# A convolution and a whitening pass: y written over x in four tiles, and pieces of one image in the last pass

## The chip, the cores and the metric

The kernel runs on one core of one Trainium2 chip. The metric is the device time of one execution in microseconds. Five engines work side by side: TensorE (PE in the profile), VectorE (DVE), ScalarE (ACT), GpSimd (POOL) and SyncE (SP). SP only issues DMAs here; 16 DMA engines move the bytes.

## The reference, cut to what matters

```python
# x: (4 images, 64 channels, 256, 256) float32
# layer 0: a separable filter from two small sine networks, hx and hy
k   = einsum('ijk,imk->ijmk', hx, hy)           # 256 x 256 taps per channel
y   = irfft2(rfft2(x, 512) * rfft2(k, 512) / 512)[..., :256, :256]   # causal 2-D convolution
y   = y + x * bias
# layer 1: whitening over channels
x1  = transpose(y, (1, 0, 2, 3)).reshape(64, -1)
s   = x1[:, ::9]                                # every ninth pixel
cov = s @ s.T / s.shape[1] + 0.01 * eye(64)
W   = five Newton-Schulz steps towards cov ** -0.5
out = W @ (x1 - mean(s))                        # for all pixels
```

Since the filter is an outer product, the convolution is done as two products with Toeplitz matrices, one along each image axis. The second layer needs W before the first output can be written, and W needs samples of all four images. So y goes to device memory and comes back in a last pass.

## The kernel before, in words

**Steps and groups.** The channels are cut into 8 blocks g of 8, and a step is one block of one image, (g, n): 32 steps, numbered i. The first 24 steps walk over g = 0 to 5 with all four images in each; the last eight are ordered by image, so steps 24 and 25 finish image 0, 26 and 27 image 1, 28 and 29 image 2, 30 and 31 image 3. A step has four items, one for each pair of channels c = 0, 2, 4, 6. An item needs two products; `group(first, second)` runs the first product of one item beside the second product of the item two before it. I write (i, c) for the group that starts with item (i, c). After the products, ScalarE copies the half results (line 396), and VectorE forms y = x * bias + product (`scalar_tensor_tensor`, line 399). `store` then sends the pair of channels to `y_d` in device memory (line 411).

**The order** of the engines' work is written out by hand (`manual_schedule`). All loads and the stores of y stand on SP's queue, which is worked off in order: a DMA whose wait is not over holds back all that is queued behind it. After each group come, in this order: the store of the item just finished, one load of x, perhaps a block of a Toeplitz matrix (`blocks`), and perhaps a piece of the last pass (`early`).

**Tiles.** The pool `big` holds three x tiles (tag `in`) and three y tiles (tag `out`) of 16 KB per partition each; every step takes the next of each. Three Toeplitz tiles and four sample tiles have the same size, so there are 13 slots of 16 KB. At (i, c) the x of step i + 2 is loaded, its last pair at (i + 1, 0).

**Samples and covariance.** When a step's last pair is stored, nine masked copies (`pack_ops`, line 313) are queued; VectorE takes about three of them after each group. They read the y tile, so it comes free only after them. `covariance(n)` runs on TensorE one image later, ahead of group (27, 4), (29, 4) and (31, 4), and at the end.

**The last pass.** After the chain that computes W, 32 pieces of 128 rows by 4096 pixels (2 MB) are read from `y_d`, multiplied by W on TensorE, shifted on ScalarE and VectorE in place, and stored from GpSimd's queue (line 598). A piece holds 4096 pixels of two images: its rows are the 64 channels of image 2v and the 64 of image 2v + 1. `homes` names the slot of each piece in turn; piece i + 13 is loaded (line 351) when piece i has been stored. Eight pieces are loaded in the loop at the places of `early`, which are (28, 4), (28, 6), (29, 6), (30, 4), (31, 2), (31, 4) and twice (31, 6), the other five of the first 13 right after it.

Of the kernel before, what the change touches and what calls it, by code (L numbers as in the profile page):

```python
# [37 lines left out]
F32 = mybir.dt.float32  # L38
# [6 lines left out]
NB, C, L = 4, 64, 256  # L45
P, H2 = 128, 2
EMB, ORDER = 33, 64
PIX = L * L
CG = 8
# [7 lines left out]
FP = 4096  # L57
# [8 lines left out]
def conv_whiten_kernel(ctx: ExitStack, tc: tile.TileContext, a: dict, out: bass.AP):  # L66
    nc = tc.nc
    x = a["x"]

    const = ctx.enter_context(tc.tile_pool(name="const", bufs=1))  # L70
    big = ctx.enter_context(tc.tile_pool(name="big", bufs=3))
    spool = ctx.enter_context(tc.tile_pool(name="spool", bufs=NB))
    tpool = ctx.enter_context(tc.tile_pool(name="tpool", bufs=3))
    o1pool = ctx.enter_context(tc.tile_pool(name="o1pool", bufs=4))
    dram = ctx.enter_context(tc.tile_pool(name="dram", bufs=1, space=bass.MemoryType.DRAM))
    psA = ctx.enter_context(tc.tile_pool(name="psA", bufs=8, space=bass.MemoryType.PSUM))

    y_d = [dram.tile([2 * C, PIX], F32, tag=f"y{v}", name=f"y_d{v}") for v in range(NB // 2)]
    g_d = dram.tile([P, GW], F32, tag="g", name="g_d")
    g0_d = dram.tile([2, GW], F32, tag="g0", name="g0_d")  # L80

    scratch = big.tile([P, 16, L], F32, tag="out", name="scratch")

    zw = scratch[0:EMB, 13:15, :].rearrange("p a w -> p (a w)")[:, 0 : L + P]
    nc.sync.dma_start(out=zw, in_=a["zw"])
# [8 lines left out]
    bias = const.tile([P, C], F32, tag="bias", name="bias")  # L96
    nc.scalar.dma_start(out=bias, in_=a["bias"].partition_broadcast(P))

    def new_x(g, n):
        return big.tile([P, CG, H2, L], F32, tag="in", name=f"x_{g}_{n}")  # L100

    def load_x(t, g, n, c):
        nc.sync.dma_start(
            out=t[:, c : c + 2],
            in_=x[n, g][:, c : c + 2],
        )
# [1 line left out]

    steps = [(g, n) for g in range(C // CG - 2) for n in range(NB)]
    steps += [(g, n) for n in range(NB) for g in range(C // CG - 2, C // CG)]  # L110
    loaded = {s: new_x(*s) for s in steps[:2]}
    for c in range(0, CG, 2):
        load_x(loaded[steps[0]], *steps[0], c)

    ident = const.tile([P, P], F32, tag="ident", name="ident")
    make_identity(nc, ident)
# [143 lines left out]

    def half_group(item, which):

        g, n, c, xt, yt, o1s = item
        jobs = []
        for u in range(2):
            banks = [
                psA.tile([P, L], F32, tag="psA", name=f"ph{which}_{g}_{n}_{c + u}_{m}")
                for m in range(H2)
            ]
            jobs.append((banks, (o1s[u] if which else xt[:, c + u]), toep[g][:, which, c + u, :]))  # L270
        toeplitz_alone(jobs, which)
        if which == 0:
            for u in range(2):
                o1s.append(o1pool.tile([P, H2, L], F32, tag="o1", name=f"o1_{g}_{n}_{c + u}"))
        for m in range(H2):
            for u in range(2):
                ps = jobs[u][0][m]
                if which == 0:
                    copy = nc.vector.tensor_copy if u else nc.scalar.copy
                    for to, fr in ((slice(0, HP), slice(HP, P)), (slice(HP, P), slice(0, HP))):  # L280
                        copy(o1s[u][to, m], ps[fr])  # L281
                else:
                    ch = g * CG + c + u
                    nc.vector.scalar_tensor_tensor(  # L284
                        yt[:, c + u, m], xt[:, c + u, m], bias[:, ch : ch + 1], ps,
                        ALU.mult, ALU.add,
                    )

# [32 lines left out]
    def covariance(n):  # L321
# [13 lines left out]
        nc.vector.scalar_tensor_tensor(cov, pc, 1.0 / NSAMP, cov, ALU.mult, ALU.add)  # L335


    pieces = [(v, q) for v in range(NB // 2) for q in range(PIX // FP)]


    homes = [
        {"t": (tpool, "toep"), "s": (spool, "samp"), "i": (big, "in"), "o": (big, "out")}[k]
        for k in "tssioitsoitos"
    ]

    def load_y(i):

        v, q = pieces[i]
        pool, tag = homes[i % len(homes)]
        t = pool.tile([P, FP], F32, tag=tag, name=f"yi_{v}_{q}")  # L350
        nc.sync.dma_start(out=t, in_=y_d[v][:, q * FP : (q + 1) * FP])
        return t

    def load_next():
        loaded[len(loaded)] = load_y(len(loaded))

    loaded_x, loaded = loaded, {}
    todo = []
    pending = []

# [8 lines left out]
            k = first + (part * 12 // 8 if g < C // CG - 2 else part)  # L369
            blocks[k // 4, k % 4 * 2] = (g, part)  # L370

    early = {(28, 4): 1, (28, 6): 1, (29, 6): 1, (30, 4): 1, (31, 2): 1, (31, 4): 1, (31, 6): 2}
    orders = [list(range(L // HP)), list(reversed(range(L // HP)))]

    def pack(time=math.inf):
# [5 lines left out]
    def group(first, second):  # L381

        units = []
        g1, n1, c1, x1, _, o1s1 = first
        g2, n2, c2, x2, y2, o1s2 = second
        for u in range(2):
            job2 = (bank(f"p2_{g2}_{n2}_{c2 + u}"), o1s2[u], toep[g2][:, 1, c2 + u, :])
            job1 = (bank(f"p1_{g1}_{n1}_{c1 + u}"), x1[:, c1 + u], toep[g1][:, 0, c1 + u, :])
            units.append((job1, job2))

        toeplitz_products(units, orders[0])
        orders.reverse()
        for u in range(2):
            o1 = o1pool.tile([P, H2, L], F32, tag="o1", name=f"o1_{g1}_{n1}_{c1 + u}")
            for to, fr in ((slice(0, HP), slice(HP, P)), (slice(HP, P), slice(0, HP))):
                nc.scalar.copy(o1[to], units[u][0][0][fr])  # L396
            o1s1.append(o1)
            ch = g2 * CG + c2 + u
            nc.vector.scalar_tensor_tensor(  # L399
                y2[:, c2 + u], x2[:, c2 + u], bias[:, ch : ch + 1], units[u][1][0],  # L400
                ALU.mult, ALU.add,
            )

        pack(2.5)
        store(second)

    def store(second):
        g, n, c, _, yt, _ = second
        last = (g, n) == steps[-1]
        row = n % 2 * C + g * CG + c  # L410
        nc.sync.dma_start(
            out=y_d[n // 2][row : row + 2, :].rearrange(
                "c (b p w) -> p (c b) w", p=P, w=L
            ),
            in_=yt[:, c : c + 2].rearrange("p c b w -> p (c b) w"),
        )
        if last and c == CG // 2 - 2 or not last and c == CG - 2:
            todo.extend(pack_ops(g, n, yt, slice(0, c + 2)))

    engines = mybir.EngineType  # L420
    with tc.manual_schedule(
        engines={engines.PE, engines.SP, engines.DVE, engines.Activation, engines.Pool}
    ):
        toep = {0: new_toeplitz(0)}

        for f, lo, hi in ((0, 0, 2), (0, 2, 4), (0, 4, 6), (1, 0, 2), (0, 6, 8), (1, 2, 4), (1, 4, 8)):
            for half in range(2):
                load_toeplitz(toep[0], 0, f, half, lo, hi)
        for c in range(0, CG, 2):
            load_x(loaded_x[steps[1]], *steps[1], c)  # L430
        for i, (g, n) in enumerate(steps):
            xt = loaded_x.pop((g, n))
            yt = big.tile([P, CG, H2, L], F32, tag="out", name=f"y_{g}_{n}")
            for c in range(0, CG, 2):
                item = (g, n, c, xt, yt, [])
                if g == C // CG - 1 and n > 0 and c == 4:
                    covariance(n - 1)
                if len(pending) == 2:
                    group(item, pending.pop(0))
                else:  # L440
                    half_group(item, 0)
                pending.append(item)
                if i == 0 and c == 6:

                    fold = const.tile([P, C], F32, tag="fold", name="fold")
                    nc.vector.tensor_tensor(fold, ident[:, 0:C], ident[:, C:P], ALU.add)
                    twice = const.tile([C, 2, C], F32, tag="twice", name="twice")
                    for u in range(2):
                        nc.vector.tensor_copy(twice[:, u], ident[0:C, 0:C])

                part = (c - 2) // 2 % 4
                to = i + 2 if c else i + 1
                if to < len(steps) and to > 1:
                    if part == 0:
                        loaded_x[steps[to]] = new_x(*steps[to])
                    load_x(loaded_x[steps[to]], *steps[to], 2 * part)
                if (i, c) in blocks:
                    tg, part = blocks[i, c]
                    if part == 0:
                        toep[tg] = new_toeplitz(tg)  # L460
                    lo = part % 2 * CG // 2
                    load_toeplitz(toep[tg], tg, part // 4, part // 2 % 2, lo, lo + CG // 2)
                for _ in range(early.get((i, c), 0)):
                    load_next()
        g, n, c, xt, yt, _ = pending[0]
        for item in pending:
            half_group(item, 1)
            pack(1.0)
            store(item)

        pack()
        pack_by_pe(g, n, yt, slice(CG // 2, CG))
        covariance(NB - 1)
        while len(loaded) < len(homes):
            load_next()
# [92 lines left out]


    halves = [slice(u * C, (u + 1) * C) for u in range(2)]  # L570
    for i, (v, q) in enumerate(pieces):
        yt = loaded.pop(i)
        o = out[2 * v : 2 * v + 2].rearrange("u c h w -> (u c) (h w)")[:, q * FP : (q + 1) * FP]

        part = FP if 1 < i < len(pieces) - 2 else FP // 4
        for w in range(FP // 1024):


            po = [
                psA.tile([P, 512], F32, tag="psA", name=f"po_{v}_{q}_{w}_{u}") for u in range(2)  # L580
            ]
            cols = [slice((2 * w + k) * 512, (2 * w + k + 1) * 512) for k in range(2)]
            for k in range(2):
# [73 lines left out]
```

## Time and profile before

| what | value |
|---|---|
| median of 3 runs | 918.35 us (917.23 to 919.46) |
| profiled execution, its own time | 917.19 us |
| its span | 915.2 us |
| mean granted TensorE clock | 0.946 |
| busy: TensorE, VectorE, ScalarE | 789.1, 658.2, 479.2 us |
| moved by DMA | 285.57 MB, mean 312 GB/s |
| loads of x: number, size, issue to landing | 128, 512 KB, 5.5 us |
| stores of y | 128, 512 KB, 4.2 us |
| pieces read, pieces written whole | 32 and 28, 2048 KB, 16.4 and 44.3 us |

The span runs from the first to the last instruction; the profiled execution's own time has about 2 us around it. A busy share is a mean over stages with different limits, so the stages are looked at one by one: a row of slices gives the busy tenths in 40 equal parts of the span, and a table by stage gives busy time, clock and DMA rate for chosen stretches. Idle time of an engine that does not set the end costs nothing.

### The profile page before, as it was taken

The numbers are of one execution on the slowest core, as the hardware profiler recorded it, in microseconds if no ns is written. First come the engines' busy times: TensorE is split into PE (matmuls) and PEld (weight loads), VectorE is DVE, ScalarE is ACT, GpSimd is POOL, SyncE is SP. The second block draws the span as 40 slices with busy tenths as digits, with TensorE's granted clock in tenths as the row PEclk, the third lists the DMA queues.
The fourth block names the chain that finished last, engine by engine and source line by source line (L and its number), as shares of the span: only waits on it lengthen the run. The fifth ranks groups of instructions, "written<-read, shape, count | busy, mean of one in ns | idle before, by whom it ended". The sixth has DMA issues, their size and how long they took to land.

```text
span 915.2 us, 27979 instructions
## 1 busy us (share of the span) xinstructions
PE 789.1 (86%) x11876; PEld 633.3 (69%) x11876; DVE 658.2 (72%) x882; ACT 479.2 (52%) x791; POOL 31.7 (3%) x71
## 2 busy tenths in 40 slices
PE   8999999999999999999999999997877777765500
PEld 7999999999999999999999999996311111111100
DVE  3468776877687768786878666867599999986500
ACT  2545454545454545454545444540498888866400
POOL 3000000000000000000000000000110000000010
PEclk9999999999999999999999999998699999987655
DMA  4988888798888888889997769989999999999998
GB/s 152 304 282 260 248 259 271 229 273 261 246 263 261 246 260 260 257 249 279 278 274 232 236 192 364 326 276 406 416 404 431 428 430 430 430 430 430 429 433 347
DMA packets 115499, 285.57 MB, mean 312 GB/s; under 512 B 6925, under 2 KB 89264, under 8 KB 107696
## 3 DMA queue, kind: packets, MB, share of 16 engines
q1 hardware_dynamic: 108176, 216.08, 71.0%
q0 software_dynamic: 6336, 67.11, 17.3%
q8 instruction: 94, 1.54, 0.7%
q10 hardware_dynamic: 864, 0.60, 0.2%
q14 instruction: 29, 0.24, 0.1%
HBM read 149.35 MB, written 134.42 MB: 310 GB/s over the span
## 4 chain that ended last, share of the span: by engine, by line
PE 68%; issue 15%; DVE 13%; DMA 1%; POOL 1%; ACT 0%; ACTq 0%; POOLq 0%; DVEq 0%
PE p L215 63%; DVE yi L593 12%; PE pc L327 2%; PE ph L247 1%; PE pk L295 1%; DMA mask<-in_mask_dram 1%; POOL pick L131 1%; PE po L585 1%; POOL out_dram L598 0%; DMA toep<-g_d 0%; DVE y L284 0%; PE ZY L500 0%; PE YT L500 0%; ACT L518 0%; DMA g_d<-scratch 0%
## 5 line engine op out<-in xcount | busy, mean ns | idle before, releaser
L215 PE MATMUL p<-toep,o 64*64 64x64 f32 (+3 forms) x5040 | 578.5, 284 | 0.2 <-issue 0.2
L215 PE MATMUL p<-toep,x 64*64 64x64 f32 (+3 forms) x5040 | 578.5, 284 | 0.1
L215 PEld LDWEIGHTS p<-toep,x 64*128 64x128 f32 (+1 forms) x5040 | 533.9, 166 | 23.4 <-issue 0.3
L215 PEld LDWEIGHTS p<-toep,o 64*128 64x128 f32 (+1 forms) x5040 | 535.2, 166 | 10.7 <-issue 0.4
L396 ACT COPY o<-p 64x512 f32<-64x512 f32 x504 | 292.4, 580 | 297.7 <-PE p L215 289.9
L313 DVE COPY_PREDICATED samp<-mask,y 128x448 f32<-128x448 int32 (+3 forms) x288 | 281.2, 976 | 6.6
L399 DVE SCALAR_TENSOR_TENSOR y<-x,bias,p 128x512 f32<-128x512 f32 x252 | 177.4, 743 | 138.7 <-PE p L215 138.1
L593 DVE TENSOR_SCALAR yi<-po,shift 64x512 f32<-64x512 f32 x256 | 192.0, 750 | 24.8 <-PE po L585 18.5
L585 PE MATMUL po<-yi,W 64*64 64x512 f32 x1024 | 152.4, 668 | 62.4 <-DVE yi L593 39.4
L590 ACT ACTIVATE yi<-po,shift 64x512 f32<-64x512 f32 x256 | 174.9, 683 | 43.9 <-PE po L585 36.8
L585 PEld LDWEIGHTS po<-yi,W 64*64 64x64 f32 x1024 | 36.8, 145 | 177.2 <-DVE yi L593 123.3
L598 POOL DMA_DIRECT2D out_dram<-yi x44 | 23.6, 537 | 263.2 <-DMA out_dram<-yi 115.4
L484 POOL MEMSET chain<- 64x64 f32 x1 | 0.1, 144 | 603.2 <-PE ph L247 603.2
L327 PEld LDWEIGHTS pc<-samp 128*64 128x64 f32 x464 | 14.3, 137 | 1.8 <-issue 1.0
L327 PE MATMUL pc<-samp 128*64 128x65 f32 x464 | 14.9, 223 | 0.4 <-ACT samp L304 0.4
L150 PE MATMUL busy<-idle 128*128 128x128 f32 x94 | 13.0, 301 | 0.0
L150 PEld LDWEIGHTS busy<-idle 128*128 128x128 f32 x94 | 12.4, 216 | 0.2 <-issue 0.2
L281 DVE COPY o<-ph 64x256 f32<-64x256 f32 x8 | 3.4, 421 | 9.1 <-PE ph L247 8.9
L295 PE MATMUL pk<-y,pick 128*128 128x112 f32 (+1 forms) x36 | 7.7, 388 | 2.6 <-DVE y L284 2.6
L335 DVE SCALAR_TENSOR_TENSOR cov<-pc,cov 128x65 f32<-128x65 f32 x4 | 0.9, 227 | 12.1 <-PE pc L327 12.1
L295 PEld LDWEIGHTS pk<-y,pick 128*128 128x128 f32 x36 | 7.2, 258 | 2.8 <-issue 2.7
L281 ACT COPY o<-ph 64x256 f32<-64x256 f32 x8 | 2.9, 367 | 10.0 <-PE ph L247 9.9
(81 smaller groups left out, 80.3 us busy)
## 6 DMA issues: line engine op xcount, KB each, us to landing
x<-in_x_dram SPq DMA_DIRECT2D x128, 512.0 KB, 5.5
y_d<-y SPq DMA_DIRECT2D x128, 512.0 KB, 4.2
yi<-y_d SPq DMA_DIRECT2D x32, 2048.0 KB, 16.4
out_dram<-yi POOLq DMA_DIRECT2D x28, 2048.0 KB, 44.3
out_dram<-yi POOLq DMA_DIRECT2D x16, 512.0 KB, 9.8
toep<-g_d SPq DMA_DIRECT2D x29, 256.0 KB, 6.6
toep<-g_d SPq DMA_DIRECT2D x29, 192.0 KB, 5.8
toep<-g_d SPq DMA_DIRECT2D x6, 128.0 KB, 3.2
```

Of the source, the lines that this page charges most:

```text
L131: nc.gpsimd.tensor_scalar(pick[:, s, :], ident, rows[:, s : s + 1], None, ALU.mult)
L150: nc.tensor.matmul(p, lhsT=idle[:, 0:P], rhs=idle[:, P : 2 * P], start=True, stop=True)
L215: mm = nc.tensor.matmul(ps[q : q + w, m, HP * k : L], lhsT=src[parts, k // 2, m * P + q : m * P + q + w], rhs=t[parts, : stop : -1] if k e ...
L295: nc.tensor.matmul(pk[:, b, :, 0:nj], lhsT=pick[:, (s - b) % STEP, :], rhs=yt[:, cs, b, s : s + STEP * (nj - 1) + 1 : STEP], start=(s == 0 ...
L313: nc.vector.copy_predicated(dst, m, src)
L327: nc.tensor.matmul(pc[half], lhsT=samp[n][:, b, j, 0:C], rhs=samp[n][:, b, j, :], start=(b == 0 and j < 2), stop=(b == H2 - 1 and j >= NJ ...
L396: nc.scalar.copy(o1[to], units[u][0][0][fr])
L399: nc.vector.scalar_tensor_tensor(y2[:, c2 + u], x2[:, c2 + u], bias[:, ch : ch + 1], units[u][1][0], ALU.mult, ALU.add,)
L585: nc.tensor.matmul(po[u][halves[k]], lhsT=W[halves[u]], rhs=yt[halves[u], cols[k]], start=True, stop=True,)
L590: nc.scalar.activation(yt[halves[0], cols[k]], po[0][halves[k]], AF.Identity, bias=shift[halves[k]])
L593: nc.vector.tensor_scalar(yt[halves[1], cols[k]], po[1][halves[k]], shift[halves[k]], None, ALU.add)
L598: nc.gpsimd.dma_start(out=o[:, end - part : end], in_=yt[:, end - part : end])
```

## The change

The pool `big` becomes `xpool` with four tiles and `epool` with two. The multiply-add of VectorE writes y over x in the same tile (the argument `yt` goes). Step i works in place i % 4 up to step 26, and in place i % 3 from step 27 on, so that the fourth tile is free for a piece. At (i, c) the pair c of step i + 2 is loaded up to step 24; step 25 loads none; from step 26 on pair c of step i + 1 is loaded. `y_d` becomes one tensor for each image, with 64 channels of the upper and 64 of the lower half as its 128 rows, so a store of two channels becomes two DMAs, one for each half, and a piece holds one image. `homes` gets the two `extra` slots first. Nine pieces are loaded in the loop, the first two at (26, 4) and (26, 6), and four right after it. The output tensor has the same order of rows, and the host puts the halves back in place after the device has finished.

```diff
-    big = ctx.enter_context(tc.tile_pool(name="big", bufs=3))
+    xpool = ctx.enter_context(tc.tile_pool(name="xpool", bufs=4))
+    epool = ctx.enter_context(tc.tile_pool(name="epool", bufs=2))
...
-    y_d = [dram.tile([2 * C, PIX], F32, tag=f"y{v}", name=f"y_d{v}") for v in range(NB // 2)]
+    y_d = [dram.tile([H2 * C, PIX // H2], F32, tag=f"y{n}", name=f"y_d{n}") for n in range(NB)]
...
+    x_tiles = {
+        u: xpool.tile([P, CG, H2, L], F32, tag="in", name=f"x{u}") for u in (3, 2, 0, 1)
+    }
+
+    def place_of(i):
+        return i % 4 if i < 27 else i % 3
...
-    pieces = [(v, q) for v in range(NB // 2) for q in range(PIX // FP)]
+    pieces = [(n, q) for n in range(NB) for q in range(PIX // H2 // FP)]
...
-        for k in "tssioitsoitos"
+        for k in "eeitssistiits"
...
-    early = {(28, 4): 1, (28, 6): 1, (29, 6): 1, (30, 4): 1, (31, 2): 1, (31, 4): 1, (31, 6): 2}
+    early = {
+        (26, 4): 1, (26, 6): 1, (27, 0): 1, (27, 2): 1, (27, 6): 1, (29, 6): 1, (31, 0): 1, (31, 4): 2
+    }
...
             nc.vector.scalar_tensor_tensor(
-                y2[:, c2 + u], x2[:, c2 + u], bias[:, ch : ch + 1], units[u][1][0],
+                x2[:, c2 + u], x2[:, c2 + u], bias[:, ch : ch + 1], units[u][1][0],
                 ALU.mult, ALU.add,
             )
...
-        row = n % 2 * C + g * CG + c
-        nc.sync.dma_start(
-            out=y_d[n // 2][row : row + 2, :].rearrange(
-                "c (b p w) -> p (c b) w", p=P, w=L
-            ),
-            in_=yt[:, c : c + 2].rearrange("p c b w -> p (c b) w"),
-        )
+        for b in range(H2):
+            row = b * C + g * CG + c
+            nc.sync.dma_start(
+                out=y_d[n][row : row + 2, :].rearrange("c (p w) -> p c w", w=L),
+                in_=yt[:, c : c + 2, b],
+            )
...
-                part = (c - 2) // 2 % 4
-                to = i + 2 if c else i + 1
-                if to < len(steps) and to > 1:
-                    if part == 0:
-                        loaded_x[steps[to]] = new_x(*steps[to])
-                    load_x(loaded_x[steps[to]], *steps[to], 2 * part)
+
+                to = i + 2 if i < 25 else i + 1
+                if i != 25 and to < len(steps):
+                    load_x(x_tiles[place_of(to)], *steps[to], c)
...
-        o = out[2 * v : 2 * v + 2].rearrange("u c h w -> (u c) (h w)")[:, q * FP : (q + 1) * FP]
+        o = out[n].rearrange("b c f -> (b c) f")[:, q * FP : (q + 1) * FP]
```

More of the change, by code (lines that the diff above doesn't have):

```diff
@@ L76, in conv_whiten_kernel @@
     psA = ctx.enter_context(tc.tile_pool(name="psA", bufs=8, space=bass.MemoryType.PSUM))
-    y_d = [dram.tile([2 * C, PIX], F32, tag=f"y{v}", name=f"y_d{v}") for v in range(NB // 2)]
+    y_d = [dram.tile([H2 * C, PIX // H2], F32, tag=f"y{n}", name=f"y_d{n}") for n in range(NB)]
     g_d = dram.tile([P, GW], F32, tag="g", name="g_d")
     g0_d = dram.tile([2, GW], F32, tag="g0", name="g0_d")
-    scratch = big.tile([P, 16, L], F32, tag="out", name="scratch")
+    scratch = epool.tile([P, 16, L], F32, tag="extra", name="scratch")
     zw = scratch[0:EMB, 13:15, :].rearrange("p a w -> p (a w)")[:, 0 : L + P]
@@ L97, in conv_whiten_kernel @@
     nc.scalar.dma_start(out=bias, in_=a["bias"].partition_broadcast(P))
-    def new_x(g, n):
-        return big.tile([P, CG, H2, L], F32, tag="in", name=f"x_{g}_{n}")
     def load_x(t, g, n, c):
@@ L110, in conv_whiten_kernel @@
     steps += [(g, n) for n in range(NB) for g in range(C // CG - 2, C // CG)]
-    loaded = {s: new_x(*s) for s in steps[:2]}
+    x_tiles = {
[3 more added lines that the diff above has]
+        return i % 4 if i < 27 else i % 3
     for c in range(0, CG, 2):
-        load_x(loaded[steps[0]], *steps[0], c)
+        load_x(x_tiles[0], *steps[0], c)
     ident = const.tile([P, P], F32, tag="ident", name="ident")
@@ L261, in half_group @@
     def half_group(item, which):
-        g, n, c, xt, yt, o1s = item
+        g, n, c, xt, o1s = item
         jobs = []
@@ L284, in half_group @@
                     nc.vector.scalar_tensor_tensor(
-                        yt[:, c + u, m], xt[:, c + u, m], bias[:, ch : ch + 1], ps,
+                        xt[:, c + u, m], xt[:, c + u, m], bias[:, ch : ch + 1], ps,
                         ALU.mult, ALU.add,
@@ L335, in covariance @@
         nc.vector.scalar_tensor_tensor(cov, pc, 1.0 / NSAMP, cov, ALU.mult, ALU.add)
-    pieces = [(v, q) for v in range(NB // 2) for q in range(PIX // FP)]
+    pieces = [(n, q) for n in range(NB) for q in range(PIX // H2 // FP)]
     homes = [
-        {"t": (tpool, "toep"), "s": (spool, "samp"), "i": (big, "in"), "o": (big, "out")}[k]
-        for k in "tssioitsoitos"
+        {"t": (tpool, "toep"), "s": (spool, "samp"), "i": (xpool, "in"), "e": (epool, "extra")}[k]
+        for k in "eeitssistiits"
     ]
     def load_y(i):
-        v, q = pieces[i]
+        n, q = pieces[i]
         pool, tag = homes[i % len(homes)]
-        t = pool.tile([P, FP], F32, tag=tag, name=f"yi_{v}_{q}")
-        nc.sync.dma_start(out=t, in_=y_d[v][:, q * FP : (q + 1) * FP])
+        t = pool.tile([P, FP], F32, tag=tag, name=f"yi_{n}_{q}")
+        nc.sync.dma_start(out=t, in_=y_d[n][:, q * FP : (q + 1) * FP])
         return t
@@ L355, in load_next @@
         loaded[len(loaded)] = load_y(len(loaded))
-    loaded_x, loaded = loaded, {}
+    loaded = {}
     todo = []
@@ L383, in group @@
         units = []
-        g1, n1, c1, x1, _, o1s1 = first
-        g2, n2, c2, x2, y2, o1s2 = second
+        g1, n1, c1, x1, o1s1 = first
+        g2, n2, c2, x2, o1s2 = second
         for u in range(2):
@@ L407, in store @@
     def store(second):
-        g, n, c, _, yt, _ = second
+        g, n, c, yt, _ = second
         last = (g, n) == steps[-1]
-        row = n % 2 * C + g * CG + c
-        nc.sync.dma_start(
-            out=y_d[n // 2][row : row + 2, :].rearrange(
-                "c (b p w) -> p (c b) w", p=P, w=L
-            ),
-            in_=yt[:, c : c + 2].rearrange("p c b w -> p (c b) w"),
-        )
+        for b in range(H2):
[4 more added lines that the diff above has]
+            )
         if last and c == CG // 2 - 2 or not last and c == CG - 2:
@@ L429, in conv_whiten_kernel @@
         for c in range(0, CG, 2):
-            load_x(loaded_x[steps[1]], *steps[1], c)
+            load_x(x_tiles[1], *steps[1], c)
         for i, (g, n) in enumerate(steps):
-            xt = loaded_x.pop((g, n))
-            yt = big.tile([P, CG, H2, L], F32, tag="out", name=f"y_{g}_{n}")
+            xt = x_tiles[place_of(i)]
             for c in range(0, CG, 2):
-                item = (g, n, c, xt, yt, [])
+                item = (g, n, c, xt, [])
                 if g == C // CG - 1 and n > 0 and c == 4:
@@ L464, in conv_whiten_kernel @@
                     load_next()
-        g, n, c, xt, yt, _ = pending[0]
+        g, n, c, yt, _ = pending[0]
         for item in pending:
@@ L570, in conv_whiten_kernel @@
     halves = [slice(u * C, (u + 1) * C) for u in range(2)]
-    for i, (v, q) in enumerate(pieces):
+    for i, (n, q) in enumerate(pieces):
         yt = loaded.pop(i)
-        o = out[2 * v : 2 * v + 2].rearrange("u c h w -> (u c) (h w)")[:, q * FP : (q + 1) * FP]
+        o = out[n].rearrange("b c f -> (b c) f")[:, q * FP : (q + 1) * FP]
         part = FP if 1 < i < len(pieces) - 2 else FP // 4
@@ L579, in conv_whiten_kernel @@
             po = [
-                psA.tile([P, 512], F32, tag="psA", name=f"po_{v}_{q}_{w}_{u}") for u in range(2)
+                psA.tile([P, 512], F32, tag="psA", name=f"po_{n}_{q}_{w}_{u}") for u in range(2)
             ]
@@ L651 @@
         ).ap()
-    out = nc.dram_tensor("out_0_dram", (NB, C, L, L), F32, kind="ExternalOutput").ap()
+    out = nc.dram_tensor("out_0_dram", (NB, H2, C, PIX // H2), F32, kind="ExternalOutput").ap()
     with tile.TileContext(nc) as tc:
@@ L655 @@
     r = run_bass_kernel_spmd(nc, [arrays], core_ids=[0])
-    return r.results[0]["out_0_dram"]
+    y = np.asarray(r.results[0]["out_0_dram"]).reshape(NB, H2, C, PIX // H2)
+    return np.ascontiguousarray(y.transpose(0, 2, 1, 3)).reshape(NB, C, L, L)
```

## The prediction

> **What bounds the kernel now.** I read the page's slices first, then the chain of waits, then busy time by stage, and last the DMA issues around the first early pieces. The slices show two regimes:
>
> ```profile
> PE   8999999999999999999999999997877777765500
> PEclk9999999999999999999999999998699999987655
> DMA  4988888798888888889997769989999999999998
> GB/s 152 304 282 260 248 259 271 229 273 261 246 263 261 246 260 260 257 249 279 278 274 232 236 192 364 326 276 406 416 404 431 428 430 430 430 430 430 429 433 347
> ```
>
> A slice is 22.9 us. Up to slice 27 TensorE is full and the DMA is not; after it the DMA stands at 430 GB/s and TensorE waits. The chain dates the borders (start, length, what):
>
> ```profile
> 521.36 3.64 PE pc L327 x116
> 525.00 36.77 PE p L215 x640
> 561.77 3.65 PE pc L327 x116
> ...
> 615.84 3.81 PE ph L247 x35
> ...
> 650.17 5.40 PE po L585 x24
> ```
>
> The two pc blocks are the covariances of images 0 and 1, ahead of group (27,4) and (29,4); (i,c) is the group of step i, channel pair c. The 36.77 us between them hold eight groups: 4.60 us a group. So group (26,4) ends near 521.36 - 3 x 4.60 = 507.6. Convolution ends at 615.8, and the last pass starts at 650.2. By stage (us, busy of PE, PEld, DVE, ACT, POOL, then clock, DMA share, GB/s):
>
> ```profile
> 500.00:525.00 25.00, 25.00 (x472) 23.38 (x468) 17.91 (x22) 12.31 (x22) 0.00 (x0) 1.00 0.76 234
> 550.00:570.00 20.00, 20.00 (x387) 18.62 (x387) 12.19 (x17) 7.27 (x13) 0.00 (x0) 1.00 1.00 376
> 600.00:605.00 5.00, 5.00 (x104) 4.54 (x103) 3.44 (x4) 2.44 (x5) 0.00 (x0) 1.00 0.44 151
> 620.00:625.00 5.00, 2.43 (x24) 2.06 (x22) 5.00 (x12) 0.00 (x0) 0.00 (x0) 1.00 0.97 359
> 625.00:630.00 5.00, 5.00 (x26) 5.00 (x26) 4.76 (x8) 0.00 (x0) 0.00 (x0) 0.66 1.02 436
> 640.00:650.00 10.00, 6.26 (x30) 4.40 (x30) 2.94 (x16) 0.82 (x4) 0.00 (x0) 0.50 1.01 433
> 650.00:660.00 10.00, 10.00 (x66) 3.35 (x67) 7.46 (x11) 7.07 (x11) 2.33 (x4) 0.71 1.00 412
> 660.00:680.00 20.00, 17.02 (x110) 4.00 (x104) 19.39 (x27) 19.46 (x29) 3.20 (x6) 1.00 1.01 394
> 680.00:900.00 220.00, 125.51 (x854) 29.50 (x854) 165.32 (x221) 148.41 (x218) 17.04 (x32) 0.86 1.01 430
> 900.00:915.20 15.20, 0.00 (x0) 0.00 (x0) 0.00 (x0) 0.00 (x0) 1.07 (x2) 0.50 0.75 307
> ```
>
> At 500-525, where y and x flow but no pieces, the DMA has a quarter to spare. At 550-570, with two pieces in the queue, it is full at 376 GB/s. From 620 to the end it is never idle. The last rows give the work left at 650: 4.12 + 7.88 + 94.6 + 4.67 = 111.3 MB. The pass moves 64 times 2.097 MB (32 pieces in, 32 out), so 53.06 were left and 10.94 pieces were in. Thirteen slots exist: the DMA was 2.06 pieces, 10.0 us at 430, behind what the slots allow. That is what earlier pieces could win.
>
> What a piece does to an x load behind it on SP's queue, first in 554.9-560, last line in 485-550 (issue to landing in us at the end):
>
> ```profile
> yi<-y_d SPq DMA_DIRECT2D x1, 2048.0 KB, 13.9
> ...
> x<-in_x_dram SPq DMA_DIRECT2D x1, 512.0 KB, 12.6
> ...
> x<-in_x_dram SPq DMA_DIRECT2D x14, 512.0 KB, 5.0
> ```
>
> Two pieces ahead turn 5.0 into 12.6. Today that is free: an x load is issued about seven groups before its use.
>
> **The change, part by part.**
>
> *In place, four tiles, steps 0 to 26.* The multiply-add on VectorE writes the same 128x512 (743 ns), so it costs nothing more. The x load of (i+2,c) now reuses step i-2's place. It waits for that step's stores, long landed, and at c=0 for its last mask copies, some 3.9 us behind the group's end (549.16 + 3.09 against a group end near 548.4 at the like place). Behind it on SP stand only toeplitz blocks and the next group's store, which waits for VectorE until 5.5 us after this end anyway. Lead is still eight groups, 37 us, over 3.9 + 5.5: cost 0. If the cover were gone, each step would lose up to 3.9 us.
>
> *Stores split in two.* 128 more issues on SP:
>
> ```profile
> L411 SPq DMA_DIRECT2D y_d<-y x128: 360/377/383, 32.0 to 624.8; - x128
> SPq L411 <- DVE y L399: 369.0, 125, 7.8
> ```
>
> 0.377 us each is 48 us of SP, inside the 369 us in which SP waits for VectorE; x loads leave 0.4 us later. Rows stay at 1 KB. The Trainium skill, "DMA: Bandwidth & Descriptors", section "Rules for kernel authors", speaks against it: at least 1 MiB per DMA for bandwidth. Its fixed 2 us ("Anatomy of one DMA", stated for GpSimd's DMAs) would make 128 x 2.0 = 256 us if each stood alone. The trace overlaps them (the 192 KB toeplitz blocks land in 5.8 us, the 512 KB x loads in 5.5), so fixed cost is latency, and nobody waits for a store but piece 0. Between 0 and 256 I take 0, with 1 us in the range for extra packets.
>
> *Pieces of one image.* Same 128 rows of 16 KB, 32 pieces, 13 slots; the work per piece (6.19 us on VectorE) is unchanged. Image 0 is stored two steps before the pair, so pieces start at (26,4), not (28,4), and nine instead of eight are issued inside the loop. Row pitch halves to 128 KB; at 430 GB/s already, I take no change (bounds -1 to +1 us).
>
> *One step of lead.* From step 26 on, x(i+1,c) is loaded at (i,c). From the end of (i,c) to the start of (i+1,c) lie three groups, 13.8 us, or 17.4 with a covariance. Pieces 0 to 3 are issued behind four consecutive groups, (26,4) to (27,2), and piece 4 behind (27,6). Take the queue as first in, first out, as the 12.6 us show, at the 376 GB/s of the mixed stage. Add 1.0 us from group end to store issue and 2.3 us fixed (5.0 us landing less some 2.7 us for the 1.05 MB of a store and a load). Counted from the end of (26,4):
> - x(28,4) stands behind five groups' y and x (5 x 1.05 MB) and four pieces (8.39 MB): 13.6 MB, 36.3 us, lands at 39.6. TensorE wants it after seven groups and a covariance, 7 x 4.60 + 3.64 = 35.8. Late by 3.8.
> - x(29,0) has two more groups and piece 4: 17.8 MB, 47.4 us, lands at 50.7; wanted at 45.0. Late by 5.7 in all, 1.9 more.
> - x(29,2): one more group, 2.8 us, against 4.6: no further stall.
>
> So TensorE waits about 5.7 us around steps 28 and 29, and everything after it, the start of the last pass too, is as late. Ends: at 430 GB/s nothing; at 352 (this view over 560-580) 8.9 us.
>
> *The clock.* After TensorE's gap of some 4.8 us at 619.7-624.5 the row 625-630 has clock 0.66: 1.7 us lost. By that row each of two waits could cost 1.7, and the stall would be 9 us. The Trainium skill, "TensorE: Matmul & The Clock Gate", Part 1, says that the clock halves only after a whole idle window of about 3.4 us, free-running: waits of 3.8 and 1.9 us seldom hold one. I take 0, and 3.4 as the upper end.
>
> *The last pass.* After the loop four slots remain instead of five (a step-30 place, the last x, the last toeplitz, the last sample tile). They come free as before, some 625 to 637 plus the shift, need 19.5 us, and all 13 are in when the pass starts. That takes the 10.0 us off. But now the DMA runs dry. The first store goes out 4.1 us after 650.2; until piece 0's place is written out, near 663, there are six quarters of 1.2 us for 8.7 us; the next read and write leave another 1 to 2 us. About 7 to 7.5 us idle. The weak rows 650-680 (2.1 us below 430) partly overlap this. Gain 10.0 - 7.2 = 2.8; between 1 and 5.
>
> **Sum.** 915.2 + 5.7 - 2.8 = 918.1 span, +2.9. The profiled execution took 917.19 (span and 2.0 around it), 1.2 under the median; added to the median, 918.35 + 2.9 = 921.2. The measurement tells from no change about 0.2%, 1.8 us: limits 916.5 and 920.2.
>
> **The rivals.**
> 1. *The queue keeps up: faster.* If the mix runs above about 427 GB/s (17.8 MB in 45.0 - 3.3 us), or x loads are served past pieces, there is no wait and the gain of 3 remains: 915.5. The last pass reaches 430, but on long rows; the mixed row says 376. With a gain of 5: 913.5. Chance 0.20.
> 2. *Hidden anyway.* A stall of 2 to 4 us against a gain near 3: 916.5 to 920. Chance 0.21.
> 3. *My case:* stall 4.5 to 9, +2 to +7 us: 0.47.
> 4. *Stall with half clock,* or slots late so that the gain is lost too: +7 to +12, 925 to 930. For it: the 0.66 row; against: the lengths of the waits. Chance 0.10.
> 5. *Not what it says:* if sharing one tile were taken as a conflict between all its channels, TensorE would wait in each of 126 groups for 1.5 us or more, +190 us. Against it: VectorE now writes one pair of y while the pair before is being stored (3.9 us), and no wait of its on that store shows. Chance 0.02.
>
> Range: 915.0 to 928.0 leaves out some 0.1 at each end. Faster 0.20, same 0.21, slower 0.59.
>
> **What would show it.** In the changed profile: pieces from about 508; TensorE waits for DMA x between 535 and 560, some 4 us before (28,4) and 2 before (29,0), none before step 27; x landing up to 15-20 us there; the end of convolution near 621.5 and the start of the pass near 656; DMA below full just before and after that start, then 430 to the end. No TensorE wait on x in steps 27 to 30 would prove the stall wrong; a pass (from its start to the end) shorter by less than 1 or more than 5 us than the 265.0 of now would prove the gain wrong.

## The result and the profile after

| | before | after |
|---|---|---|
| median | 917.11 us (11 runs) | 921.21 us (11 runs) |
| ratio of after to before, 95% interval | | 1.004 (1.003 to 1.005) |
| span of the profiled execution | 915.2 us | 919.6 us |
| convolution ends | 615.8 | 621.1 |
| last pass starts | 650.2 | 655.6 |
| last pass, start to end | 265.0 | 264.0 |

The change makes the kernel slower by 0.4%, some 4 us. In the profiles, 5.2 us are lost in the convolution, in steps 28 and 29, and the last pass gives 1 us back.

The chain of waits after the change (start, length, what), to be read beside that of before:

```profile
522.02 3.64 PE pc L332 x116
525.67 4.58 PE p L220 x64
530.25 1.40 DVE x L406 x2
531.66 0.37 SPq L419
532.08 14.48 DMA y_d<-x
546.63 11.33 DMA x<-in_x_dram
558.10 9.55 PE p L220 x158
567.65 3.65 PE pc L332 x116
571.29 36.78 PE p L220 x632
608.08 3.64 PE pc L332 x116
...
621.07 3.77 PE ph L252 x35
...
655.57 3.69 PE po L588 x16
```

From 530 to 558 the chain leaves TensorE, where before there was nothing else on it: a store of y takes 14.48 us to land, then a load of x, that of (29,0), takes 11.33, and TensorE goes on with it. The load is the eighth DMA that SP issues after this store, and SP sends it off just as the store has landed (546.56 and 546.63); run 2 below asks whether this hold on SP is the cause. Between the starts of the covariances of images 0 and 1 now lie 45.63 us; before it was 40.41. The loss of 5.22 us sits between these two marks: outside them, 0.66 us more before the first and 0.67 less up to the next (40.43 against 41.10) cancel.

VectorE's multiply-add comes right after each group's matmuls, so its starts are the clock of the groups (start, length, operation, in brackets the idle time before and what ended it). First the kernel before, then after; the rows are (28,2), (28,4), (28,6) and (29,0):

```profile
542.91 1.40 DVE L399 SCALAR_TENSOR_TENSOR y<-x,bias,p 128x512 f32<-128x512 f32 x2
547.84 1.41 DVE L399 SCALAR_TENSOR_TENSOR y<-x,bias,p 128x512 f32<-128x512 f32 x2 [3.53 <-PE p L215]
552.15 1.40 DVE L399 SCALAR_TENSOR_TENSOR y<-x,bias,p 128x512 f32<-128x512 f32 x2
556.98 1.40 DVE L399 SCALAR_TENSOR_TENSOR y<-x,bias,p 128x512 f32<-128x512 f32 x2 [0.48 <-PE p L215]
```

```profile
544.31 1.61 DVE L406 SCALAR_TENSOR_TENSOR x<-x,bias,p 128x512 f32<-128x512 f32 x2 [0.64 <-PE p L220]
552.66 1.41 DVE L406 SCALAR_TENSOR_TENSOR x<-x,bias,p 128x512 f32<-128x512 f32 x2 [6.74 <-PE p L220]
556.97 1.41 DVE L406 SCALAR_TENSOR_TENSOR x<-x,bias,p 128x512 f32<-128x512 f32 x2
562.87 1.41 DVE L406 SCALAR_TENSOR_TENSOR x<-x,bias,p 128x512 f32<-128x512 f32 x2 [1.55 <-PE p L220]
```

The step to (28,4) grew from 4.93 to 8.35 us, that to (29,0) from 4.83 to 5.90. The step to (28,2) grew by 0.73; the row ahead of it, not shown, starts at 538.69 before and 539.36 after. Sum: 0.73 + 3.42 + 1.07 = 5.22 us. TensorE's own timeline names what it waited for at all three places:

```profile
540.31 0.24 PE L220 MATMUL p<-toep,x 64*64 64x64 f32 x1 [0.68 <-DMA x<-in_x_dram]
547.94 0.45 PE L220 MATMUL p<-toep,x 64*128 64x256 f32 x1 [2.82 <-DMA x<-in_x_dram]
558.10 0.45 PE L220 MATMUL p<-toep,x 64*128 64x256 f32 x1 [0.64 <-DMA x<-in_x_dram]
```

These waits add up to 4.1 us; the trace names no wait for the other 1.1.

By stage (us, busy of PE, PEld, DVE, ACT, POOL, clock, DMA share, GB/s):

```profile
540.00:550.00 10.00, 6.87 (x97) 6.33 (x99) 5.10 (x7) 4.10 (x8) 0.00 (x0) 1.00 1.03 410
655.00:660.00 5.00, 5.00 (x26) 1.92 (x30) 2.38 (x4) 2.12 (x4) 0.26 (x1) 0.55 0.14 59
660.00:665.00 5.00, 5.00 (x45) 1.66 (x38) 4.84 (x8) 4.86 (x8) 2.07 (x4) 1.00 0.72 285
665.00:670.00 5.00, 5.00 (x29) 1.24 (x26) 4.86 (x7) 4.87 (x8) 1.60 (x3) 1.00 0.88 342
670.00:680.00 10.00, 7.84 (x57) 1.87 (x56) 9.69 (x14) 9.73 (x15) 1.07 (x2) 1.00 1.00 360
680.00:900.00 220.00, 128.05 (x886) 29.79 (x878) 170.48 (x228) 153.35 (x225) 17.08 (x32) 0.89 1.01 428
900.00:919.60 19.60, 0.00 (x0) 0.00 (x0) 0.00 (x0) 0.00 (x0) 1.60 (x3) 0.50 0.76 313
```

In 540-550 TensorE waits while the DMA is busy all the time (share 1.03) at 410 GB/s: what TensorE waits for is at its limit. The clock stays 1.00. In 655-660, around the start of the last pass, the DMA share is 0.14, where it was 1.00 before (row 650-660 in the prediction): every slot is loaded, and no finished piece is there to be stored.

### The profile page after: what moved, and what is told of

It reads as the page before. It is cut to its first block, busy times and chain, and to the rows that moved or that the text cites. A ratio compares the mean times of both kernels' runs of the same rounds, so it can differ in the third digit from the quotient of the medians.

```text
span 919.6 us, 28167 instructions
## 1 busy us (share of the span) xinstructions
PE 788.6 (86%) x11876; PEld 633.1 (69%) x11876; DVE 658.0 (72%) x882; ACT 479.2 (52%) x791; POOL 31.7 (3%) x71
## 4 chain that ended last, share of the span: by engine, by line
PE 65%; issue 15%; DVE 13%; DMA 4%; POOL 1%; ACT 0%; ACTq 0%; POOLq 0%; SPq 0%; DVEq 0%
PE p L220 60%; DVE yi L596 12%; PE pc L332 2%; DMA y_d<-x 2%; DMA x<-in_x_dram 1%; PE ph L252 1%; PE pk L300 1%; DMA mask<-in_mask_dram 1%; POOL pick L136 1%; POOL out_dram L601 0%; PE po L588 0%; DMA toep<-g_d 0%; DVE x L289 0%; PE ZY L503 0%; PE YT L503 0%
## 5 line engine op out<-in xcount | busy, mean ns | idle before, releaser
L318 DVE COPY_PREDICATED samp<-mask,x 128x448 f32<-128x448 int32 (+3 forms) x288 | 280.9, 975 | 6.6
L406 DVE SCALAR_TENSOR_TENSOR x<-x,bias,p 128x512 f32<-128x512 f32 x252 | 177.3, 742 | 144.1 <-PE p L220 143.5
L588 PE MATMUL po<-yi,W 64*64 64x512 f32 x1024 | 150.4, 657 | 63.1 <-DVE yi L596 40.9
L300 PE MATMUL pk<-x,pick 128*128 128x112 f32 (+1 forms) x36 | 7.9, 398 | 2.5 <-DVE x L289 2.5
L300 PEld LDWEIGHTS pk<-x,pick 128*128 128x128 f32 x36 | 7.5, 304 | 2.7 <-issue 2.7
```

The lines of the kernel that those rows point to most:

```text
L300: nc.tensor.matmul(pk[:, b, :, 0:nj], lhsT=pick[:, (s - b) % STEP, :], rhs=yt[:, cs, b, s : s + STEP * (nj - 1) + 1 : STEP], start=(s == 0 ...
L318: nc.vector.copy_predicated(dst, m, src)
L406: nc.vector.scalar_tensor_tensor(x2[:, c2 + u], x2[:, c2 + u], bias[:, ch : ch + 1], units[u][1][0], ALU.mult, ALU.add,)
L588: nc.tensor.matmul(po[u][halves[k]], lhsT=W[halves[u]], rhs=yt[halves[u], cols[k]], start=True, stop=True,)
```

## The experiments

My theory (A): four pieces in a row fill SP's queue, and x with one step of lead comes too late behind them. Rivals: the doubled number of stores holds SP back (B); the tiles in place cost something in every step (C). For the gain: it is capped because all 13 slots are full at the start of the last pass and the DMA then idles. Each ratio below is to the kernel before, run beside it, with medians of 917.2 to 917.9 us.

**1. The same nine pieces, spread out.**

```diff
-        (26, 4): 1, (26, 6): 1, (27, 0): 1, (27, 2): 1, (27, 6): 1, (29, 6): 1, (31, 0): 1, (31, 4): 2
+        (26, 4): 1, (27, 0): 1, (27, 6): 1, (28, 6): 1, (29, 6): 1, (30, 4): 1, (31, 0): 1, (31, 4): 2
```

> The changed kernel with its nine early pieces kept and only spread out: behind (26,4), (27,0), (27,6), (28,6), (29,6), (30,4), (31,0) and twice (31,4). Theory A (bytes: four pieces in a row fill SP's queue, and x loads with one step of lead land too late): no TensorE wait on x, convolution ends 5.2 us earlier than in the changed kernel (near 615.8), total 916 us, about 1 us under the kernel before. Theory B (the doubled number of stores: a DMA on SP waits for the one eight issues earlier, so SP itself holds the x loads back): the stores are still doubled, so some of the wait stays, 918 to 921. Theory C (in-place tiles cost something in every step): 921, unchanged.

Measured: 916.08 us, ratio to before 0.9984 (0.9976 to 0.9992). The chain has TensorE alone again:

```profile
525.36 36.87 PE p L220 x639
562.23 3.64 PE pc L332 x116
...
615.69 3.77 PE ph L252 x35
...
649.76 5.40 PE po L588 x24
```

The stall is gone with nothing but the places of the pieces changed, while the stores are still doubled and the tiles still in place. So C falls, B cannot be the cause alone, and A holds so far.

**2. One store instead of two.**

```diff
-        for b in range(H2):
-            row = b * C + g * CG + c
-            nc.sync.dma_start(
-                out=y_d[n][row : row + 2, :].rearrange("c (p w) -> p c w", w=L),
-                in_=yt[:, c : c + 2, b],
-            )
+        row = 2 * (g * CG + c)
+        nc.sync.dma_start(
+            out=y_d[n][row : row + 4, :].rearrange("r (p w) -> p r w", w=L),
+            in_=yt[:, c : c + 2].rearrange("p c b w -> p (c b) w"),
+        )
```

> The changed kernel with one store for two channels instead of two, as in the kernel before. For that the rows of y_d are interleaved (channel, half), so the last pass multiplies the wrong rows together; the work is the same. Theory A (bytes): the wait at steps 28 and 29 stays, 921 within 1 us. Theory B (SP held back by the count of DMAs): the x loads are issued up to 3 us earlier and the wait falls from 5.2 us to 2 or less, 917 to 918.

Measured: 921.12 us, 1.0040 (1.0024 to 1.0056), as the changed kernel. In its profile 44.34 us lie between the covariances, so 3.9 of 5.2 us of the stall stay. The load of (29,0) stands on the chain here too, now without a store ahead of it:

```profile
543.89 12.99 DMA x<-in_x_dram
```

SP sends it off 2.7 us earlier than in the changed kernel (543.89 against 546.63), but it lands only 1.1 us earlier (556.88 against 557.96): with the DMA full, leaving earlier helps a load little when the same bytes stand ahead of it. So B falls as the main cause; at most 1.3 us of the stall could be owed to the number of stores. No run lifts SP's hold altogether.

**3. Before, with stores in two.**

```diff
-        nc.sync.dma_start(
-            out=y_d[n // 2][row : row + 2, :].rearrange(
-                "c (b p w) -> p (c b) w", p=P, w=L
-            ),
-            in_=yt[:, c : c + 2].rearrange("p c b w -> p (c b) w"),
-        )
+        for b in range(H2):
+            nc.sync.dma_start(
+                out=y_d[n // 2][row : row + 2, b * PIX // 2 : (b + 1) * PIX // 2].rearrange(
+                    "c (p w) -> p c w", w=L
+                ),
+                in_=yt[:, c : c + 2, b],
+            )
```

> The kernel before with each store split into two of 256 KB, one for each half, nothing else. The prediction's step (128 more issues on SP cost nothing): 917.1 within 1 us. Rival (count of DMAs in flight matters, or small DMAs are slower): 919 or more, with TensorE waits on x or a lower DMA rate in steps 28 to 31.

Measured: 916.78 us, 0.9990 (0.9984 to 0.9997). The split, 256 stores of half the size for 128, costs nothing.

**4. Eight early pieces instead of nine.**

```diff
-        (26, 4): 1, (26, 6): 1, (27, 0): 1, (27, 2): 1, (27, 6): 1, (29, 6): 1, (31, 0): 1, (31, 4): 2
+        (26, 4): 1, (26, 6): 1, (27, 0): 1, (27, 2): 1, (27, 6): 1, (29, 6): 1, (31, 0): 1, (31, 4): 1
```

> The changed kernel with one early piece less (one instead of two behind (31,4)), so eight as before. Theory A with the slots as limit (all 13 are in before the pass starts and the DMA then idles for some 6 us): a piece that comes later fills the idle time, so the total stays 921 within 1 us. Rival (every piece loaded in the loop is worth its 4.9 us of DMA): 925 to 926.

Measured: 922.50 us, 1.0048 (1.0032 to 1.0065), against 1.004 (1.003 to 1.005) of the changed kernel; the intervals overlap. Its last pass is 263.2 us long (655.7 to 918.9). The ninth piece does not bring 4.9 us: loaded later, it falls into time in which the DMA would idle anyway.

**5. The nine early pieces on ScalarE's queue.**

```diff
-        nc.sync.dma_start(out=t, in_=y_d[n][:, q * FP : (q + 1) * FP])
+        (nc.scalar if i < 9 else nc.sync).dma_start(out=t, in_=y_d[n][:, q * FP : (q + 1) * FP])
```

> The changed kernel with its nine early pieces issued from ScalarE's queue instead of SP's, at the same places. Theory A1 (the x loads are late because SP's queue is first in, first out, and four pieces stand ahead): on another queue the DMA engines take turns, x lands within 10 us, and the wait at steps 28 and 29 falls below 1 us: 916 us. Theory A2 (it is the bytes: the DMA engines are full for 35 us whatever the queue): x gets at most half of the rate, so part of the wait stays: 918 to 921. A cost of its own (ScalarE's copies wait behind a piece's issue) would show as TensorE waits on banks.

Measured: 927.33 us, 1.0103 (1.0088 to 1.0118). Both forms of the theory missed: it got much worse. The DMAs issued in 505-510 (median of issue to landing at the end):

```profile
yi<-y_d ACTq DMA_DIRECT2D x1, 2048.0 KB, 10.8
x<-in_x_dram SPq DMA_DIRECT2D x2, 512.0 KB, 26.3
y_d<-x SPq DMA_DIRECT2D x2, 256.0 KB, 20.3
```

A load of 512 KB on SP's queue takes 26 us while a piece of 2 MB on the other lands in 11. The two queues don't share evenly: from 510 to 536 the piece queue, with rows of 16 KB, moved 8.1 MB, and SP's, with rows of 1 and 4 KB, 2.2 MB. One queue, worked off in order, was the milder case. The slow load is the x of (27,4), which TensorE got in time in the changed kernel. There the first piece was issued behind it, at 512.2; here it left before it, at 508.3. Now this x comes 11 us late, and the last pass starts 7.6 us later than there (at 663.2).

**6. Three pieces at once, with one step of lead.**

```diff
-        (26, 4): 1, (26, 6): 1, (27, 0): 1, (27, 2): 1, (27, 6): 1, (29, 6): 1, (31, 0): 1, (31, 4): 2
+        (26, 4): 3, (27, 6): 1, (28, 6): 1, (29, 6): 1, (31, 0): 1, (31, 4): 2
```

> The changed kernel with three pieces at once behind (26,4) and the others later: (27,6), (28,6), (29,6), (31,0), twice (31,4). One step of lead as in the changed kernel. Theory A (burst against one step of lead, by the prediction's count of bytes): only x of (27,6), issued right behind the three pieces and wanted three groups later, is late, by about 4 us; convolution ends near 619.5, total 919.5. Rival (any wait needs the four pieces in a row): no wait, 916.

Measured: 923.22 us, 1.0055 (1.0042 to 1.0067). The place is as expected, the total 3.7 us above it. Its DMA issues in 513-517, VectorE's row for (27,6), and the clock (third column from the end) from the wait on:

```profile
x<-in_x_dram SPq DMA_DIRECT2D x1, 512.0 KB, 20.0
```

```profile
540.11 1.64 DVE L406 SCALAR_TENSOR_TENSOR x<-x,bias,p 128x512 f32<-128x512 f32 x2 [6.15 <-PE p L220]
```

```profile
530.00:534.50 4.50, 0.00 (x0) 0.02 (x1) 3.89 (x5) 2.01 (x4) 0.00 (x0) 1.00 1.05 396
534.50:537.00 2.50, 2.49 (x46) 2.40 (x48) 0.00 (x0) 0.00 (x0) 0.00 (x0) 0.61 1.07 404
```

The x issued at 514.4 lands 20.0 us later, and TensorE waits 4.6 us for it, near the 4 expected. Then it works at clock 0.61, and the group grew by 6.2 us in all (its row is 10.5 us after the one before; the same group of the next run, with two steps of lead, takes 4.3). That slower work behind the wait is what I had not counted; it makes up some 2 us of the difference.

**7. The same three pieces at once, with two steps of lead.**

```diff
-        return i % 4 if i < 27 else i % 3
+        return i % 4
...
-                to = i + 2 if i < 25 else i + 1
-                if i != 25 and to < len(steps):
+                to = i + 2
+                if to < len(steps):
...
-        u: xpool.tile([P, CG, H2, L], F32, tag="in", name=f"x{u}") for u in (3, 2, 0, 1)
+        u: xpool.tile([P, CG, H2, L], F32, tag="in", name=f"x{u}") for u in (0, 1, 2, 3)
...
-        for k in "eeitssistiits"
+        for k in "eetssiistiits"
...
+        (26, 4): 3, (27, 6): 1, (29, 6): 1, (30, 2): 1, (31, 2): 1, (31, 4): 2
```

> Step i in place i % 4 to the end, so x is loaded two steps ahead throughout; the four x places come free later and the early pieces stand behind (26,4) three times, (27,6), (29,6), (30,2), (31,2) and twice (31,4), again nine. Theory A (the lead is what makes a burst cost): the same three pieces at once as in the run with one step of lead now cost nothing, convolution ends near 615.8, total 916. Rival (a burst costs by itself, whatever the lead): 919 or more.

The later pieces had to move too, but the wait of run 6 came before any of them. Measured: 915.72 us, 0.9975 (0.9964 to 0.9986). Its x issued in 513-517 is as slow, and the chain does not notice:

```profile
x<-in_x_dram SPq DMA_DIRECT2D x1, 512.0 KB, 20.2
```

```profile
525.12 36.76 PE p L220 x640
561.88 3.64 PE pc L332 x116
```

20.2 us against 20.0, once free and once 6 us. Lead decides what a burst costs.

**8. Two steps of lead, pieces one by one.** As 7, with `early` (26, 4), (26, 6), (27, 0), (27, 6), (29, 6), (30, 2), (31, 2), twice (31, 4).

> As the last, two steps of lead to the end, with the pieces behind (26,4), (26,6), (27,0), (27,6), (29,6), (30,2), (31,2) and twice (31,4). Theory A: no wait on x, total 916, the same as with the pieces spread out, since the last pass starts with all 13 slots full and the DMA idle in both. Rival (earlier pieces still win something): 914 to 915.

Measured: 915.10 us, 0.9976 (0.9963 to 0.9989). Better than both kernels; no different from 7 and, by the intervals, from 1.

**9. Twelve slots.** From 1, with:

```diff
-    epool = ctx.enter_context(tc.tile_pool(name="epool", bufs=2))
+    epool = ctx.enter_context(tc.tile_pool(name="epool", bufs=1))
...
-        for k in "eeitssistiits"
+        for k in "eitssistiits"
...
+        (26, 4): 1, (27, 0): 1, (27, 6): 1, (28, 6): 1, (29, 6): 1, (31, 0): 1, (31, 4): 2
```

> The kernel with the pieces spread out, with 12 slots in the last pass instead of 13: one of the two extra slots is gone, and eight pieces are early. No wait on x is expected in either. Theory (the last pass starts with every slot full and the DMA idle, so its length is set by how many pieces the slots hold): one piece more, 4.9 us of DMA, is left at the start, 920 to 922. Rival (the idle DMA at the start takes it up, slots don't matter): 916.

Measured: 921.89 us, 1.0043 (1.0030 to 1.0056); run 1, with thirteen, had 0.9984. The pass takes 268.8 us (651.8 to 920.6) against 263.2 (649.8 to 913.0). It also starts 2.0 us later, which the slots do not explain; about half of that is a pause in the covariance of image 1 for which the trace names nothing. Around the start of the pass the DMA has spare time in both; two rows with twelve slots, then one with thirteen:

```profile
650.00:655.00 5.00, 4.76 (x22) 2.29 (x26) 1.73 (x5) 1.24 (x2) 0.00 (x0) 0.50 0.31 131
655.00:660.00 5.00, 5.00 (x40) 1.59 (x36) 4.54 (x7) 4.25 (x8) 1.79 (x3) 0.72 0.52 207
```

```profile
650.00:655.00 5.00, 5.00 (x28) 1.37 (x24) 3.00 (x4) 2.73 (x4) 0.73 (x1) 0.50 0.02 10
```

So the pass starts with the slots full and a DMA that has little to do, and its length goes with the number of slots: taking one away costs 5.6 us, while a piece loaded earlier (4) brings nothing.

## Why the prediction was right, and where it was off

- *The stall in steps 28 and 29* carried the forecast, and it holds by 1, 6 and 7. The count of bytes gave 3.8 us up to (28,4) and 1.9 more at (29,0), 5.7 in all; measured 4.15 (0.73 at (28,2) and 3.42) and 1.07, 5.2 in all. I had not listed (28,2): by the same count its x lands at 31.2 and is wanted at 31.2, on the edge. The mix ran at 398 to 433 GB/s in the 10 us rows from 520 to 550, faster than the 376 assumed, but the first piece was issued only at 512.2, some 3 us later than I had it. The two errors cancel in part, so it is partly luck that the size came out so close. I also had x of (29,0) leave about 1 us after its group; it left 7 us after VectorE began that group's work (539.36 to 546.63): the mask copies read its tile until 543.7, and SP was behind. That the landing time still fits is because the DMA was full all along. The slow loads of x landed in 10 to 13 us, not 15 to 20.
- *What I set at zero* was zero: tiles in place and the load two steps ahead (1 has them and no stall), split stores (3). The Trainium skill's demand for DMAs of at least 1 MiB ("DMA: Bandwidth & Descriptors", "Rules for kernel authors") therefore does not price these stores: TensorE waits for none of them. SP does: in the changed kernel it waits for earlier DMAs of its own, up to 2.5 us at a time, and a store stands on the chain for that reason, but by run 2 this is not the main part of the stall.
- *The clock.* In the rows from 500 to 620 of the changed kernel's profile it stayed at 1.00, with waits of 0.68, 2.82 and 0.64 us. That agrees with the whole idle window of about 3.4 us that the Trainium skill ("TensorE: Matmul & The Clock Gate", Part 1) asks for before the clock halves. Run 4 does not agree: its wait before (28,4) is no longer, and there the clock fell (TensorE's row and two stage rows of run 4):

```profile
547.84 0.45 PE L220 MATMUL p<-toep,x 64*128 64x256 f32 x1 [2.67 <-DMA x<-in_x_dram]
546.50:550.00 3.50, 2.16 (x13) 1.81 (x15) 0.00 (x0) 0.29 (x1) 0.00 (x0) 0.79 1.12 454
550.00:555.00 5.00, 5.00 (x105) 4.62 (x101) 0.67 (x2) 0.57 (x1) 0.00 (x0) 0.81 0.96 387
```

  The measurement decides: a wait of 2.67 us was enough there, less than the window (from the last matmul's start to the next one's it is 3.1 us), so my reason for taking 0 does not hold, and that the changed kernel's profile shows a full clock is partly luck. It would have cost little. In run 4 the step to (28,4) took 9.98 us instead of 8.35, but (29,0) then had no wait left, and 46.02 us lie between the covariances against 45.63: most of what the slower clock cost was taken back at the next place where TensorE would have waited for the DMA.
- *The gain of the last pass* is the step that was mis-sized: 2.8 expected (between 1 and 5), 1.0 measured. The rows shown from 655 on hold 107.3 MB, 51.2 transfers instead of 53.06: 9.1 us saved, not 10.0. Against 430 GB/s the rows 655-680 lose 8.6 us; the rows 650-680 of before lost 2.1. The difference of 6.5 is near my 7.2. Up to here 2.6 us would be left. What I had not counted is behind it: 428 instead of 430 GB/s in the long middle, 1.0 us, and a tail that loses 5.3 us (6.13 MB in 19.6 us) instead of 4.3 (4.67 MB in 15.2), another 1.0. I took the tail as unchanged. What makes it longer was not tested. The other profiles that start the pass with all 13 slots full have 263.1 to 263.6 us, 1.4 to 1.9 under before, and run 3, whose pass is that of before, has 264.2 instead of 265.0. So one profile fixes the gain only to about 1 us. The runs without a stall (1, 7, 8) say more: their medians lie 1.5 to 2.3 us under before, by the ratios. The gain is real, and probably smaller than the 2.8 forecast.
- *The sum:* 5.2 - 1.0 in place of 5.7 - 2.8. Both terms have the sign forecast; the smaller gain makes it 4 instead of 3 us. That the median of 921.2 is the very number forecast is luck: I added 2.9 us to 918.35, the median of three runs, and measured 4.1 us on 917.11, that of eleven.
- *The rivals:* "the queue keeps up" falls by the waits in the trace, "not what it says" by 1, whose chain has no wait of TensorE on a tile in steps 26 to 31.

## What to carry to other kernels

Giving a buffer away for an earlier prefetch shortens the lead of the loads that shared it. Count the bytes that stand ahead of such a load on its queue, divide by the rate of that stage, and compare with the time to its use; as many prefetches, spread out (1) or with the lead kept (7), cost nothing. And ask what an earlier prefetch can win: here all slots were full when the last pass began, so a still earlier piece brings nothing; one slot less cost 5.6 us (9), and one more was not tried.

## What the runs showed of the hardware that I had not expected

Moving bulk loads to another queue did not protect the small ones: with 2 MB pieces of 16 KB rows on ScalarE's queue, a 512 KB load on SP's took 26.3 us, where the slow ones of the changed kernel took 13.1. That rows or packets of different length cause the uneven share is a guess; it was not tried with shorter rows. A wait of 4.6 us for x came before a TensorE clock of 0.61 in the next 2.5 us (6). A wait of 2.67 us came before 0.79 and 0.81 (4), and one of 2.82 us, in the changed kernel with the same burst, left the clock at 1.00; what decides between the two is open.
